# Window attention and a factored convolution, two layers in one kernel: a second layout for the value table, and the statistics rows loaded one unit later

## The chip, the cores and the metric

The kernel runs on one core of one Trainium2 chip. The metric is the device time of one execution in microseconds (us). Three executions of the kernel before gave 2969.43, 2971.66 and 2973.84 us; their median, 2971.66 us, is the time before.

## The reference, cut to what matters

The input x has 2 images of 128 channels and 256 x 256 pixels, float32. Two layers follow each other, each with a group norm in front and a residual around it:

```
x = x + attention(gn(x))          # layer 0
x = x + convolutions(gn(x))       # layer 1
```

`gn` takes mean and variance over 4 channels and the whole image, so an image's statistics must be complete before its first row can be normalised. The attention cuts the image into windows of 8 x 8 pixels (the queries) and reads keys and values from the 12 x 12 pixels around each (the 8 x 8 and a border of 2), with 4 heads of 32 channels, a relative position term, and a mask:

```
qkv  = W_qkv @ gn(x)
q    = 8x8 windows of q;  k, v = 12x12 windows of k, v (stride 8)
attn = softmax(q k^T * scale + rel_pos(q) + mask)     # mask: -inf unless row and column offset are both odd
out  = W_out @ (attn v)
```

The mask lets a query see only those keys whose row and column differ from its own by odd numbers. The kernel uses that: it splits rows and columns by parity and computes only what the mask leaves. Layer 1 (a 5 x 1 convolution, a 3 x 1 channelwise one, a product with a 1 x 3 dilated one) is not touched by the change.

## The kernel before, in words

An image is cut into 32 strips of 8 rows. A strip is worked on in two *units*, one for each row parity r; unit u belongs to strip k = u // 2 and parity r = u % 2. Two images give 64 strips and 128 units. A strip's 256 columns are 32 windows, taken as 16 pairs (`NPAIR = 16`); the column parity is called c. Below, an *even unit* has r = 0, an *odd unit* r = 1, and the two units of one strip are a *pair of units*.

Layer 0 (`attention_fast`) emits its instructions under a manual schedule: for each of the five engines (TensorE, VectorE, ScalarE, GpSimd, SyncE) the order in which the code emits is the order in which the engine runs. Only semaphores, set by the framework from what each instruction reads and writes, hold an instruction back. The loop over u emits in this order:

- even unit: `load_rows(k + 2)` (L316, the rows of a later strip, 10 rows = 1280 KB); odd unit: `normalise(k + 2)` (L356 on VectorE);
- in the first image, at the even units 2, 4, ... 58: `input_stats(u)` (L128 `bn_stats` on VectorE over 8 or 10 rows of the second image, tile `f_sx`) and right after it `load_next()` (L305, the next 8 or 10 rows of the second image into the same single buffer `f_sx`). The second image's group norm is thereby prepared during the first;
- `biases(u)` (L562) and `scores(u)` (L579) on TensorE, the exponentials on ScalarE (L589);
- `keys(u + 1)` (L382, `f_pk`), `coefficients` (L473, L482, L486);
- `attend(u)`: for each of 16 window pairs and 4 heads one matmul (L605, `f_o`), whose moving operand is a slice of the value table `f_vt`: 128 keys, 2 column parities, 33 values (32 channels and a 1 that gives the softmax's denominator);
- in an odd unit: `bring(1, ...)`; `turn(u)`;
- in an even unit: `values(k + 1)` (L495, `f_pv`, 4 groups of 4 matmuls into the row buffer `f_vn`, copied at L500) and `bring(0, ...)`; in an odd unit: the queries of the next two units (L445, L447, `f_pq`);
- `project(u)` (L382, `f_py`; L639 adds the residual; L643 stores the result of the unit, 512 KB, to DRAM).

All of layer 0's loads and stores are issued by SyncE (SPq in the profile), in the order emitted. Its completion counters are eight, used in rotation: in the compiled order each transfer waits for the one issued eight places before it, besides what its buffers ask for.

The value table. `f_vn` holds a strip's value rows, one partition for each of 128 pixel positions (32 for each of r and c), all 16 window pairs behind each other in the free dimension: 16 x 4 heads x 33 floats = 8,448 bytes. `f_vt[r]` holds, for one row parity, the keys of a window: partitions 0 to 63 for column parity 0, 64 to 127 for column parity 1, and the other column parity's places stay zero, so that one matmul gives both column parities side by side. `bring(r, pieces)` moves a strip's rows from `f_vn` to `f_vt[r]` with DMAs from SBUF to SBUF: for each c and piece, the rows themselves (L525), and the two border columns, taken from the neighbouring pair (L529, L532). A window's 6 key rows of one parity lie in a ring, so a strip's 4 rows are one piece (4 rows) in two strips out of three and two pieces (2 and 2) in the third. `bring` thus issues 6 DMAs in two strips out of three and 12 in the third; I call the pairs of units *light* and *heavy* for it. `bring_top` (L542, L546, L549) does the same for the two rows above an image's first strip.

TensorE's program is fully unrolled; matmuls in float32 appear in the profile as two weight loads (PEld) and two matmuls (PE) each. `PIECES` and `pieces(u)` cut some matmuls into parts and are the same in both kernels.

The shape of the table and the order of its dimensions are one line (L221), the place of the load another (L685):

```
vt = [cst.tile([P, NPAIR, 2, HEADS, 33], F32, ...) for r in range(2)]
...
if u == 0 or u in stats_at:
    load_next()
```

Of the kernel before, what the change touches and what calls it, by code (L numbers as in the profile page):

```python
# [10 lines left out]
F32 = mybir.dt.float32  # L11
# [9 lines left out]
P = 128  # L21
W = 256
HEADS = 4
# [4 lines left out]
NPAIR = 16  # L28
# [159 lines left out]
def attention_fast(tc, io, x1_d, norm, st_x, st_y, tags, ends, weights, both, layer1):  # L188

    nc = tc.nc  # L190
# [4 lines left out]
    with ExitStack() as l0:  # L195
        cst = l0.enter_context(tc.tile_pool(name="f_cst", bufs=1))
# [21 lines left out]
        xo = [t[:, 2048:2560].rearrange("p (n r c j) -> p n r c j", n=NPAIR, r=2, c=2) for t in xt]  # L218
        tops = {}
        kt = [cst.tile([P, 2, NPAIR * NKEY + 4], F32, tag=f"f_kt{r}", name=f"f_kt{r}") for r in range(2)]  # L220
        vt = [cst.tile([P, NPAIR, 2, HEADS, 33], F32, tag=f"f_vt{r}", name=f"f_vt{r}") for r in range(2)]  # L221
        vn = both.sb.tile([P, NPAIR, HEADS, 33], F32, tag="vn", name="f_vn")

        sc = [
# [6 lines left out]
        for r in range(2):  # L231
            nc.gpsimd.memset(kt[r], 0.0)
            nc.gpsimd.memset(vt[r], 0.0)
            for c in range(2):
                nc.gpsimd.memset(vt[r][64 * c : 64 * c + 64, :, c, :, 32:33], 1.0)
        nc.gpsimd.memset(vn[..., 32:33], 1.0)
        nc.gpsimd.memset(wb, 0.0)

# [43 lines left out]
        stats_at, norm_at = {}, {}  # L282
        quarter_at = {}
        for b in range(NB - 1):
            row = 0
            for i in range(NS - 3):
                n = 10 if i < 12 else 8
# [23 lines left out]
        def load_rows(k):  # L311

            b, s = divmod(k, NS)
            t = rawp.tile([P, 10, W], F32, tag="raw", name=f"f_raw_{k}")
            n = min(10, H - 8 * s)
            nc.sync.dma_start(t[:, 0:n, :], x[b, :, 8 * s : 8 * s + n, :])  # L316
            raws[k] = t

        def slots_of(k):

            first = (4 * k + 2) % 6
            return [(0, 4, first)] if first < 4 else [(0, 2, 4), (2, 2, 0)]
# [195 lines left out]
        def bring(r, pieces):  # L518

            end = NPAIR - 1  # L520
            for c in range(2):
                at, to = 32 * (2 * r + c), 64 * c
                for i, m, slot in pieces:
                    lo = at + 8 * i
                    nc.sync.dma_start(  # L525
                        vt[r][to + 8 * slot : to + 8 * (slot + m), :, c], vn[lo : lo + 8 * m]
                    )
                    first = to + 48 + 2 * slot
                    nc.sync.dma_start(  # L529
                        vt[r][first : first + 2 * m - 1 : 2, 1:NPAIR, c], vn[lo + 7 : lo + 8 * m : 8, 0:end]  # L530
                    )
                    nc.sync.dma_start(  # L532
                        vt[r][first + 1 : first + 2 * m : 2, 0:end, c], vn[lo : lo + 8 * m - 7 : 8, 1:NPAIR]
                    )

        def bring_top(r, b):

            v, slot = tops[b][2], 4 * NS * b % 6
            for c in range(2):
                for odd in range(2):  # L540
                    lo, to = 64 * odd + 16 * (2 * r + c), 64 * c
                    nc.sync.dma_start(  # L542
                        vt[r][to + 8 * slot : to + 8 * slot + 16, odd:NPAIR:2, c], v[lo : lo + 16]
                    )
                    first = to + 48 + 2 * slot
                    nc.sync.dma_start(  # L546
                        vt[r][first : first + 3 : 2, odd + 1 : NPAIR : 2, c], v[lo + 7 : lo + 16 : 8, 0 : 8 - odd]
                    )
                    nc.sync.dma_start(  # L549
                        vt[r][first + 1 : first + 4 : 2, 1 - odd : NPAIR - 1 : 2, c],  # L550
                        v[lo : lo + 9 : 8, 1 - odd : 8],
                    )

# [40 lines left out]
        def attend(u):  # L594
            p = pts.pop(u)
            ons[0] = on = wk.tile([P, 2, NPAIR, 32], F32, tag="on", name=f"f_on_{u}", bufs=1)
            k, r = divmod(u, 2)
            if r == 0:
                rcs[0] = wk.tile([P, 2, NPAIR, 2, 1], F32, tag="rc", name=f"f_rc_{k}")
            for lo, hi in ((0, 6), (6, 11), (11, NPAIR)):  # L600
                bank = ps_pj.tile([P, 512], F32, tag="pj", name=f"f_o_{u}_{lo}")
                po = bank[:, 0 : 66 * (hi - lo)].rearrange("p (n c d) -> p n c d", c=2, d=33)
                for n in range(lo, hi):
                    for h in range(HEADS):
                        nc.tensor.matmul(  # L605
                            po[32 * h : 32 * h + 32, n - lo], p[:, h // 2, n, h % 2],
                            vt[r][:, n, :, h], start=True, stop=True,
                        )

                rc = rcs[0][:, r, lo:hi]  # L610
                nc.vector.reciprocal(rc, po[:, :, :, 32:33])
                nc.vector.tensor_tensor(
                    on[:, :, lo:hi].rearrange("p c n d -> p n c d"), po[:, :, :, 0:32],
                    rc.to_broadcast([P, hi - lo, 2, 32]), ALU.mult,
                )
# [35 lines left out]
        def emit(parts):  # L651
            for f in parts:
                f()
# [4 lines left out]
        with tc.manual_schedule(engines=ORDERED):  # L658
            normalise(0)
            emit(keys(0, ONE, ONE))  # L660
            top_values(0)
            bring_top(0, 0)
            values(0, range(4))
            for r in range(2):
                bring(r, slots_of(0))
            bring_top(1, 0)
            by_place(0, (0, 4))
            coefficients(0, 0)
            coefficients(0, 1)
            normalise(1)  # L670
            by_place(1, (0, 2))
            for u in range(2):
                emit(queries(u, ONE, ONE))
            for u in range(NU):
                k, r = divmod(u, 2)
                b, s = divmod(k, NS)
                later, more = u + 1 < NU, k + 1 < NB * NS
                if r == 0:
                    if k + 2 < NB * NS:
                        load_rows(k + 2)  # L680
                elif k + 2 < NB * NS:
                    normalise(k + 2)
                if u in stats_at:
                    input_stats(u)
                if u == 0 or u in stats_at:  # L685
                    load_next()
                step = lambda: None
                if u in norm_at:
                    st, i, name = norm_at[u]
                    steps = norm.steps(st[i], ps_pj, name, last=False)  # L690
                    step = lambda: next(steps)
                if u == 8:
                    weights.sums()
                if u in (NU - 4, NU - 2, NU - 1):
                    next(layer1)
                biases(u)
                scores(u, pieces(u)[3])
                step()
                step()
                at_top = more and (k + 1) % NS == 0  # L700
                cuts = pieces(u)[0]
                if later:
                    emit(keys(u + 1, cuts, cuts))
                step()
                step()
                if more:
                    coefficients(k + 1, r)
                elif later:
                    next(layer1)
                step()  # L710
                attend(u)
                if more and r == 1:
                    bring(1, slots_of(k + 1))
                    if at_top:
                        bring_top(1, b + 1)
                if not later:
                    next(layer1)
                turn(u)
                step()
                if r == 0 and more:  # L720
                    if at_top:
                        top_values(b + 1)
                        bring_top(0, b + 1)
                    values(k + 1, range(4))
                    bring(0, slots_of(k + 1))
                elif later and more:
                    cuts = pieces(u)[1]
                    emit(queries(u + 1, cuts, cuts) + queries(u + 2, cuts, cuts))
                if more and r == 0:
                    by_place(k + 1, (2, 4))  # L730
                elif k + 2 < NB * NS:
                    by_place(k + 2, (0, 2))
                if u > 0:
                    result_stats(u - 1)
                project(u)
                if u in quarter_at:
                    st, i, name, part = quarter_at[u]
                    norm.quarter(st[i], name, part)
                del qs[u]
            result_stats(NU - 1)  # L740
# [966 lines left out]
```

## Time and profile before

| What | Value |
|---|---|
| median of 3 executions | 2971.66 us |
| profiled execution, its own time | 2972.91 us |
| span in that profile (first to last instruction) | 2971.0 us |
| granted TensorE clock | 0.994 |
| PE busy | 2785.4 us (94%) |
| DVE busy | 2136.9 us (72%) |
| ACT busy | 1509.7 us (51%) |
| POOL busy | 640.7 us (22%) |
| layer 0's first `f_o` matmul / last | 119.5 us / 1973.5 us |

The profile is of one execution, 1.9 us longer than its span and 1.25 us over the median. Up to about 91 us the statistics of the first image are loaded; the units of the first image run from about 112 to 1069 us, those of the second to 1976 us, layer 1 from there on. A line of the view of waits reads: engine, what it was about to do, what ended the wait, then total us, number of times and the longest. "issue" stands for idle time for which the profile shows no wait on anything. A line of the timeline reads: start, duration, engine, line of code, operation, tiles, number of instructions merged, and in brackets the idle time before it.

### The profile page before, as it was taken

The page shows a single profiled execution, that of the slowest core. Times are in us where ns is not written, and L with a number is a line of the kernel's source. Part 1 is how long each engine was busy: PE and PEld are TensorE (multiplying, and loading weights), DVE is VectorE, ACT ScalarE, POOL GpSimd, SP SyncE. Part 2 cuts the span into 40 slices and gives each one's busy share as a digit, 9 for nine tenths or more (in the row PEclk, how much of TensorE's full clock was granted, in tenths as well). Part 3 has the DMA queues.
Part 4 walks back from the last instruction along what each step waited for, and adds up shares of the span by engine and source line. Part 5 has one row for each costly group of instructions (what it writes and reads, how often), then busy time and mean ns, then how long its engine had stood idle before and what let it go on. Part 6 is the DMA issues. An engine that isn't in the chain of part 4 may idle for free.

```text
span 2971.0 us, 117385 instructions
## 1 busy us (share of the span) xinstructions
PE 2785.4 (94%) x51762; PEld 2109.1 (71%) x51762; DVE 2136.9 (72%) x3601; ACT 1509.7 (51%) x2379; POOL 640.7 (22%) x2049
## 2 busy tenths in 40 slices
PE   0699999999999999999999999999999999999998
PEld 0588888888888888989888899864444444444443
DVE  8566666666666655655556565569999999999997
ACT  0345454445444545445454554546666666666654
POOL 1233322233332332332333323300000000000000
PEclk9999999999999999999999999999999999999999
DMA  9666655566555455455454555448888878888885
GB/s 394 197 185 176 173 163 170 161 174 175 157 169 158 134 127 135 123 136 126 134 146 120 137 128 138 123 123 216 217 221 216 213 212 215 220 217 216 218 217 148
DMA packets 309396, 521.83 MB, mean 176 GB/s; under 512 B 20784, under 2 KB 259856, under 8 KB 276752
## 3 DMA queue, kind: packets, MB, share of 16 engines
q1 hardware_dynamic: 299808, 448.17, 51.0%
q0 software_dynamic: 9072, 66.06, 11.9%
q8 instruction: 412, 6.75, 0.9%
q14 instruction: 104, 0.85, 0.1%
HBM read 284.78 MB, written 134.22 MB: 141 GB/s over the span
## 4 chain that ended last, share of the span: by engine, by line
PE 76%; issue 19%; SPq 1%; POOL 1%; DMA 1%; DVE 1%; ACT 1%; POOLq 0%; DVEq 0%; ACTq 0%
PE f_s L579 9%; PE f_o L605 9%; PE f_pk L382 8%; PE f_pv L495 8%; PE f_py L382 8%; PE a_o L887 6%; PE a_e L887 6%; PE f_pq L447 6%; PE f_pa L473 4%; PE f_s L562 4%; PE f_pq L445 2%; PE a_d L938 2%; PE a_c L887 1%; PE b L980 1%; PE g L867 1%
## 5 line engine op out<-in xcount | busy, mean ns | idle before, releaser
L486 DVE TENSOR_SCALAR f_cf<-f_pa,f_keep 128x512 f32<-128x512 f32 x128 | 103.7, 810 | 546.8 <-ACT f_cf L482 546.7
L589 ACT ACTIVATE f_p<-f_s 128x512 f32<-128x512 f32 x512 | 265.4, 602 | 442.7 <-PE f_s L579 442.0
L453 ACT ACTIVATE f_q<-f_pq,f_head 128x512 f32<-128x512 f32 x512 | 303.1, 702 | 153.8 <-PE f_pq L447 153.8
L396 POOL COPY f_kt<-f_kt 128x60 f32<-128x60 f32 (+1 forms) x348 | 105.8, 340 | 1262.4 <-ACT f_kt L410 1238.6
L373 POOL COPY f_xq<-f_xn 128x96 f32<-128x96 f32 x1024 | 333.2, 356 | 12.3 <-DVE f_xn L356 12.3
L962 ACT ACTIVATE t<-t,w 128x1024 f32<-128x1024 f32 x127 | 145.9, 1149 | 368.2 <-DVE t L955 363.0
L969 DVE SCALAR_TENSOR_TENSOR t<-t,w,t 128x1024 f32<-128x1024 f32 x254 | 325.9, 1283 | 7.3 <-ACT t L962 1.3
L605 PE MATMUL f_o<-f_vt,f_p 128*32 128x66 f32 x16384 | 280.1, 222 | 34.2 <-issue 33.9
L579 PEld LDWEIGHTS f_s<-f_q,f_kt 64*64 64x64 f32 x17176 | 275.0, 133 | 52.0 <-issue 51.7
L579 PE MATMUL f_s<-f_q,f_kt 64*64 64x64 f32 (+1 forms) x17176 | 293.9, 221 | 1.5 <-issue 1.1
L605 PEld LDWEIGHTS f_o<-f_vt,f_p 128*32 128x32 f32 x16384 | 250.9, 109 | 50.8 <-issue 41.2
L495 PE MATMUL f_pv<-f_wqkvT,f_xn 128*128 128x128 f32 x2048 | 251.7, 280 | 24.0 <-issue 22.9
L495 PEld LDWEIGHTS f_pv<-f_wqkvT,f_xn 128*128 128x128 f32 x2048 | 236.2, 192 | 32.4 <-issue 25.9
L382 PE MATMUL f_pk<-f_xn,f_wqkvT 128*128 128x192 f32 (+3 forms) x1496 | 257.3, 321 | 0.7 <-ACT f_kt L410 0.7
L382 PE MATMUL f_py<-f_ot,f_woT 128*128 128x160 f32 (+1 forms) x1520 | 248.5, 313 | 7.0 <-issue 5.0
L998 POOL DMA_DIRECT2D y<-f_x x63 | 54.5, 866 | 919.1 <-DVE y L990 871.2
L887 PE MATMUL a_o<-xm,w1s 128*128 128x512 f32 x512 | 242.3, 594 | 4.5 <-ACT t L878 4.5
L887 PE MATMUL a_e<-xm,w1s 128*128 128x512 f32 x512 | 240.7, 591 | 0.0
L382 PEld LDWEIGHTS f_py<-f_ot,f_woT 128*128 128x128 f32 x1520 | 230.7, 192 | 11.6 <-issue 8.8
L382 PEld LDWEIGHTS f_pk<-f_xn,f_wqkvT 128*128 128x128 f32 x1496 | 221.3, 190 | 12.6 <-issue 1.7
L447 PE MATMUL f_pq<-f_xn,f_wq_s 128*128 128x192 f32 (+1 forms) x1008 | 210.2, 331 | 0.0
L500 ACT COPY f_vn<-f_pv 128x512 f32<-128x512 f32 x128 | 75.0, 586 | 263.2 <-PE f_pv L495 245.0
(149 smaller groups left out, 4782.8 us busy)
## 6 DMA issues: line engine op xcount, KB each, us to landing
f_raw<-in_x SPq DMA_DIRECT2D x62, 1280.0 KB
f_x<-f_x SPq DMA_DIRECT2D x128, 512.0 KB
y<-f_x POOLq DMA_DIRECT2D x63, 1024.0 KB, 7.9
out<-y SPq DMA_DIRECT2D x63, 1024.0 KB
f_sx<-in_x SPq DMA_DIRECT2D x49, 1024.0 KB
f_vt<-f_vn SPq DMA_DIRECT2D x172, 264.0 KB
raw<-f_x SPq DMA_DIRECT2D x64, 640.0 KB
raw<-f_x SPq DMA_DIRECT2D x62, 384.0 KB
```

The source lines that it names most:

```text
L373: nc.gpsimd.tensor_copy(xq[:, half, t2, 1:4, :, c].rearrange("p t r n e -> p r t n e"), xn[k % 2][:, windows, :, c, 0:3, t2:8:4].rearrange ...
L382: nc.tensor.matmul(dst[:, 512 * lo // last : 512 * hi // last], w, moving[:, n * lo // last : n * hi // last], start=True, stop=True,)
L447: nc.tensor.matmul(by_pair[:, lo:hi, 8:32], wq_s, xn[k % 2][:, lo:hi, r, c, 0:3].rearrange("p n i j -> p n (i j)"), start=True, stop=True,)
L453: nc.scalar.activation(q[:, c, :, i].rearrange("p n (j t) -> p n j t", t=4), pq.rearrange("p (n t j) -> p n j t", n=NPAIR, t=4), AF.Copy, ...
L473: nc.tensor.matmul(pa[64 * half : 64 * half + 64, 64 * t : 64 * t + 64], wb[:, t2, t1].rearrange("p h x -> p (h x)"), xq[:, half, t2, t1]. ...
L495: nc.tensor.matmul(pv[:, P * n : P * n + P], xn[k % 2][:, 4 * g + n].rearrange("p r c i j -> p (r c i j)"), wvT, start=True, stop=True,)
L579: nc.tensor.matmul(sc[g][n // 8][64 * c : 64 * c + 64, n % 8, lo:hi].rearrange("p i x -> p (i x)"), kt[r][rows, c, NKEY * n : NKEY * n + 6 ...
L589: nc.scalar.activation(pts[u][:, g, 8 * half : 8 * half + 8].rearrange("p n i x -> p (n i x)"), sc[g][half].rearrange("p n i x -> p (n i x ...
L605: nc.tensor.matmul(po[32 * h : 32 * h + 32, n - lo], p[:, h // 2, n, h % 2], vt[r][:, n, :, h], start=True, stop=True,)
L887: nc.tensor.matmul(pa[:, : n * W], w, rows, start=i == 0, stop=i == len(terms) - 1)
L962: nc.scalar.activation(t3[:, j : j + 4], t1[:, j : j + 4, :], AF.Copy, scale=w3[:, 0:1])
L969: nc.vector.scalar_tensor_tensor(t3[:, j : j + 4], t1[:, j + tap : j + tap + 4, :], w3[:, tap : tap + 1], t3[:, j : j + 4], ALU.mult, ALU.add,
```

## The change

Two edits. First, the value table's dimensions "pair" and "column parity" change places: from `[P, NPAIR, 2, HEADS, 33]` to `[P, 2, NPAIR, HEADS, 33]`. In the old order the 16 pairs of one column parity lie 1,056 bytes apart in a partition, in runs of 528 bytes; in the new order they lie behind each other. The matmul's slice follows: its two column parities now lie 8,448 bytes apart and no longer 528. Second, `load_next()` is called in the unit after one with statistics (3, 5, ... 59; in the last there is nothing left to load) and no longer in the unit itself. Neither the order nor the number of compute instructions differs, and the DMAs are as many as before.

```diff
-        vt = [cst.tile([P, NPAIR, 2, HEADS, 33], F32, tag=f"f_vt{r}", name=f"f_vt{r}") for r in range(2)]
+        vt = [cst.tile([P, 2, NPAIR, HEADS, 33], F32, tag=f"f_vt{r}", name=f"f_vt{r}") for r in range(2)]
...
-                nc.gpsimd.memset(vt[r][64 * c : 64 * c + 64, :, c, :, 32:33], 1.0)
+                nc.gpsimd.memset(vt[r][64 * c : 64 * c + 64, c, :, :, 32:33], 1.0)
...
         def bring(r, pieces):
...
-                        vt[r][to + 8 * slot : to + 8 * (slot + m), :, c], vn[lo : lo + 8 * m]
+                        vt[r][to + 8 * slot : to + 8 * (slot + m), c], vn[lo : lo + 8 * m]
...
-                        vt[r][first : first + 2 * m - 1 : 2, 1:NPAIR, c], vn[lo + 7 : lo + 8 * m : 8, 0:end]
+                        vt[r][first : first + 2 * m - 1 : 2, c, 1:NPAIR], vn[lo + 7 : lo + 8 * m : 8, 0:end]
...
-                        vt[r][first + 1 : first + 2 * m : 2, 0:end, c], vn[lo : lo + 8 * m - 7 : 8, 1:NPAIR]
+                        vt[r][first + 1 : first + 2 * m : 2, c, 0:end], vn[lo : lo + 8 * m - 7 : 8, 1:NPAIR]
...
         def bring_top(r, b):
...
-                        vt[r][to + 8 * slot : to + 8 * slot + 16, odd:NPAIR:2, c], v[lo : lo + 16]
+                        vt[r][to + 8 * slot : to + 8 * slot + 16, c, odd:NPAIR:2], v[lo : lo + 16]
...
         def attend(u):
...
-                            vt[r][:, n, :, h], start=True, stop=True,
+                            vt[r][:, :, n, h], start=True, stop=True,
...
-                if u == 0 or u in stats_at:
+                if u == 0 or u - 1 in stats_at:
                     load_next()
```

More of the change, by code (lines that the diff above doesn't have):

```diff
@@ L546, in bring_top @@
                     nc.sync.dma_start(
-                        vt[r][first : first + 3 : 2, odd + 1 : NPAIR : 2, c], v[lo + 7 : lo + 16 : 8, 0 : 8 - odd]
+                        vt[r][first : first + 3 : 2, c, odd + 1 : NPAIR : 2], v[lo + 7 : lo + 16 : 8, 0 : 8 - odd]
                     )
                     nc.sync.dma_start(
-                        vt[r][first + 1 : first + 4 : 2, 1 - odd : NPAIR - 1 : 2, c],
+                        vt[r][first + 1 : first + 4 : 2, c, 1 - odd : NPAIR - 1 : 2],
                         v[lo : lo + 9 : 8, 1 - odd : 8],
```

## The prediction, made before the changed kernel ran

> **What bounds the kernel now.** I read the page first: TensorE (PE) is the bound, and from the third of 40 slices on it is nearly full. What can be gained in layer 0 lies in PE's idle time after 130 us; the 91 us of loading ahead of it are not touched.
>
> ```profile
> PE 2785.4 (94%) x51762; PEld 2109.1 (71%) x51762; DVE 2136.9 (72%) x3601; ACT 1509.7 (51%) x2379; POOL 640.7 (22%) x2049
> PE   0699999999999999999999999999999999999998
> q1 hardware_dynamic: 299808, 448.17, 51.0%
> q8 instruction: 412, 6.75, 0.9%
> ```
>
> The view of waits for PE says what this idle time is. Over the whole run:
>
> ```profile
> PE f_o L605 <- issue: 33.9, 41, 2.3
> PE f_pv L495 <- issue: 22.9, 19, 2.2
> PE f_pq L445 <- DVE f_cf L486: 7.9, 2, 5.5
> PE f_py L382 <- issue: 5.0, 8, 1.3
> ```
>
> The reader is to see that these are some 60 us with no semaphore to blame. Split into stretches, the first image (115 to 590 and 590 to 1070 us) and then the second (1070 to 1550 and 1550 to 1990) differ in one thing. The first pair of lines below is 115:590, the second 590:1070:
>
> ```profile
> PE f_pv L495 <- issue: 15.8, 12, 2.2
> PE f_o L605 <- issue: 6.4, 9, 2.2
> ...
> PE f_o L605 <- issue: 7.1, 9, 2.0
> PE f_pv L495 <- issue: 5.9, 6, 1.7
> ```
>
> and the second image, 1070:1550 and 1550:1990:
>
> ```profile
> PE f_o L605 <- issue: 10.9, 11, 2.3
> PE f_pv L495 <- issue: 1.1, 1, 1.1
> ...
> PE f_o L605 <- issue: 9.5, 12, 2.0
> PE f_py L382 <- issue: 3.3, 5, 1.3
> ```
>
> The f_o stalls are in both images (13.5 us, then 20.4), the f_pv stalls only in the first: 21.7 us against 1.1, or 6.1 with f_py (1.7 in 1070:1550 and the 3.3 shown), where the same block of instructions ends in the second image. The first image alone has statistics loads. The timeline shows such a stall in the middle of a run of like matmuls, where no semaphore stands:
>
> ```profile
> 416.75 1.69 PE L605 MATMUL f_o<-f_vt,f_p 128*32 128x66 f32 x100 [0.30 <-issue]
> 418.37 3.17 PE L495 MATMUL f_pv<-f_wqkvT,f_xn 128*128 128x128 f32 x26
> 422.93 0.83 PE L495 MATMUL f_pv<-f_wqkvT,f_xn 128*128 128x128 f32 x6 [1.39 <-issue]
> ```
>
> From one stall to the next are 100 + 26 matmuls and as many weight loads, 252 instructions. And in nearly every pair of units the stalls sit in the even unit, in which SyncE has just issued two loads, the strip rows and the statistics rows:
>
> ```profile
> 410.99 0.63 SPq L316 DMA_DIRECT2D f_raw<-in_x  x1
> 413.32 0.33 SPq L305 DMA_DIRECT2D f_sx<-in_x  x1
> ```
>
> So I read the stall as PE waiting for its next 256 instructions. The trace's DMA packet records bear this out. Queue q8 carried 412 packets of 16 KB; PE's 103,524 matmuls and weight loads and 1,572 semaphore instructions are 410.5 times 256. The packets of these two loads ran from 413.3 to 421.3 us; instruction packets ran at 414.53 to 415.50 and 420.51 to 421.51, and PE went on at 416.75 and 422.93, 1.25 and 1.42 us after their ends. After the block boundary at 416.75 the fetch began 3.8 us later. In odd units, with no load in flight, it begins 0.8 to 2 us after the boundary and PE does not stop.
>
> **What the Trainium skill says.** "Runtime: NRT & Kernel Launch", section Instruction fetch mechanics: instructions are streamed in blocks of 16 KiB, 256 instructions, and the cost of a boundary is "mostly hidden". The block size agrees (412 packets); hidden it is not here, at up to 2.3 us a time. "DMA: Bandwidth & Descriptors", section Queues, rings and completion order: each DMA engine goes round robin between the rings it has work for, a packet at a time. The trace agrees in part: the fetch gets in before a burst is over, but late. The same page, Why small descriptors are slow, says that transfers within SBUF don't suffer from small descriptors. The trace disagrees: the 528-byte packets, all but a few from f_vn to f_vt, take 46.8 ns on average, 11 bytes/ns, and 8,192-byte ones on the same queue 368 ns, 22 bytes/ns.
>
> **The change part by part.**
>
> *Value table.* The run of 16 pairs becomes one run of 8,448 bytes (7,920 for the border columns). The trace has 164,320 packets of 528 bytes; 2,528 belong to bring_top, whose source skips every other pair, and stay. The other 161,792 (7,574 us of engine time at 46.8 ns) become 10,240 long ones. At the 368 ns of an 8,192-byte packet, scaled with size, that is about 3,840 us. So q1's share falls by 3,730/(16 x 2971) = 8 points, to about 43%. What is it worth to PE? The bring bursts (425.9 to 434.4 us, 435.6 to 444.0) lie mostly in odd units and between them, where PE has no stall, so I take 0. The work that hides it is two units' time, some 29 us, between a bring and the attend that reads it; without that cover a bring's 4 to 8 us would show. Bounds: the freed engines could shorten f_o stalls (at best half of 33.9, 17 us), or longer packets could delay fetches in odd units, as in the third rival. SyncE's issue time is 0.62 us a DMA whatever its shape and stays; the L532 issues, median 872 ns, may come down to the 621 of L525, off the path.
>
> *The matmul's slice* has 66 columns in two runs before and after. Nothing in the trace has another stride on this operand, so its cost is bounded by 0 on both sides unless the runs' distance counts; I take 0 and look at the 219 ns of L605. The four memsets of ones (0.21 us each) are at the start under the loading.
>
> *Statistics load leaves even units.* The DMAs queued behind it on SyncE, bring(0) and the store, move up by one issue, 0.33 us, and lose SyncE's waits for bn_stats (24.4 us in all, covered: bring(0) waits for f_vn ten us later anyway). On PE the f_pv stalls fall to what the second image has: 21.7 - 6.1 = 15.6 us gained. One piece of evidence from the first image itself: the last load is issued at 941.0 us; the next heavy pair has no such load and stalls 0.24 us at 978.87, where earlier heavy ones lost 1.0 to 2.2. f_o stalls stay: the strip rows are issued first, and these stalls are as long without a statistics load.
>
> *It comes into odd units*, 29 loads less the first, between the even unit's store (L643) and bring(1). In a light pair (store issued at 458.85) it would be issued near 459.5, with packets from 461.8 (2.3 us from issue to packet, as at 410.99) to about 466 (4 us for 8 rows). PE's boundaries are near 462.1 (a fifth into f_o) and 467.1 (the end of f_pq). A fetch must have begun by about 464.8 (1 us for the packet and 1.35 to PE's restart), 2.7 us after the boundary; in even units f_o to f_pv leaves 2.3. Under strip rows alone, the even unit's fetch is late by 1 us (stalls of 0.3) or, in a quarter of the cases, by 3 (stalls of 2). With the larger margin the first is free and the second costs about 1 us: 0.25 us a load. In a heavy pair the load would go out near 433.5, its packets from 436 to 440; the fetch at 439.13 is then up to 1 us late with about 0.3 to spare. I take 0.25 us again: 28 x 0.25 = 7 us lost. Bounds: 0, and 28 x 1.2 = 34 us if each stalls as an f_pv did (21.7/18).
>
> *The wait that it adds.* By the rotation of eight counters, the eighth DMA of a heavy bring(1) waits for the statistics load to land (near 441 us, its turn at 439); behind it on SyncE are four more brings, the store and the next strip load, about 2 us late. The store's buffer is wanted at the next L639, the brings by the next L500 copy, both over 3 us later: 0. VectorE wants the rows at 439.95: up to 1.5 us late, and VectorE idles 3.46 us before the f_cf that PE needs: 0; in light pairs they land some 3 us early.
>
> *Sum:* -15.6 + 7 = -8.6 us. The profiled execution's 2972.91 us becomes 2964.3; on the median, 1.25 lower, 2963.
>
> **Rivals.** *The stall only moves*: odd units lose what even ones gain, 0.55 us a load: 2971. For: the margin is only 0.4 us larger. Against: a single burst there, two now.
>
> *The compact table helps PE as well*: strip rows no longer share engines with late bring packets, f_o stalls halve: -8.6 - 17 = -25.6, 2946. For: f_o holds most of the stalls. Against: in light pairs the bring burst ends at 410.4, before the strip rows' first packet at 413.3.
>
> *Slower*: long packets in odd units. Statistics rows and 8,448-byte table rows meet in the same rings just after f_o's boundary, and each load stalls PE 1.2 us there: 34 - 15.6 = +18, 2990. It decides from 0.55 us a load, and is measurable from (15.6 + 6)/28 = 0.77. For: fetches were late only beside 8 and 10 KB packets, never beside 528-byte ones. Against: bring(1) issues one row per engine each 0.65 us or so, which leaves gaps.
>
> **How the numbers follow.** 0.2%, 6 us, is about what a measurement of this kernel can tell from no change. Forecast 0.47 (0.42 faster, 0.05 within), moved 0.24 (0.20 within, 0.04 slower), table helps too 0.12 (faster), slower 0.17. So faster 0.54, same 0.25, slower 0.21. The range runs from 2950 (all 21.7 us gone, nothing lost) to 2982 (0.9 us lost a load: 26 - 15.6 = +10); most of the slower case and half of the table's lie outside, under 0.2. The forecast's own range is 2956 to 2968.
>
> **What would show it.** Right: waits of PE in 115:1070 with f_pv under 8 us, f_o near 13.5, new stalls in odd units (f_pq, f_py, or f_s after them) under 10; second image unchanged within 5 us; q1 near 43%; L605 at 219 ns. Wrong: new odd-unit stalls over 15 us; f_o stalls that shrink in the second image, where only the table changed; a longer L605.

## The result and the profile after

The changed kernel takes 2961.39 us (median of 20 executions), the kernel before in the same sessions 2971.51 us. The ratio is 0.9967, with a 95% interval of 0.9955 to 0.9978: about 10 us faster, where 8.6 had been forecast. The profiled execution has a span of 2960.0 us, against 2971.0.

The total came out near the forecast. Its two parts did not. The view of waits for PE in the first image (115 to 1070 us) of the changed kernel:

```profile
PE f_s L579 <- issue: 19.3, 10, 4.0
PE f_pq L445 <- issue: 14.6, 8, 3.2
PE f_o L605 <- issue: 11.1, 15, 1.6
PE f_pv L495 <- issue: 4.9, 4, 2.2
PE f_pq L447 <- issue: 3.0, 5, 0.9
```

The f_pv stalls have gone as forecast, from 21.7 us to 4.9. But where 7 us were to come back through the loads in odd units, f_s and f_pq have 36.9; 3.2 of these are one stall in unit 1, ahead of the first moved load, and 33.7 are left for the loads. In the second image (1070 to 1990), where only the table changed and nothing was to happen:

```profile
PE f_o L605 <- issue: 14.5, 19, 4.1
```

The f_o stalls fell from 20.4 us, and the f_py ones, 5.0 before, are gone. Of the 14.5 us, 4.1 are one stall at the change of images, where the kernel before waited 5.5 us for VectorE; without it 10.4 are left, half of what there was.

Waits do not hold everything. The clock records show TensorE's granted clock at half, mostly for 3.41 us at a time, which costs 1.7 us each. In layer 0 of the kernel before and the changed one 12 of the 14 such stretches begin within 1.5 us of the end of a stall of 1.7 us or more; that the stall brings them on is my reading, not shown by a run of its own.

So I count in units. From the instruction records I take the first bias matmul (L562) of each unit; from one to the next a unit that never stalls takes 13.70 us in every kernel of the table below. The time over that, summed, is a kernel's loss in layer 0. I leave out the first two units, the change of images (61 to 65) and the last four. "After a heavy bring(1)" are the even units that follow an odd one with 12 brings.

| us over 13.70 a unit | 1st image: even, other | even, after a heavy bring(1) | odd | 2nd image: even | odd |
|---|---|---|---|---|---|
| before | 35.5 | 18.6 | 1.3 | 36.7 | 2.5 |
| changed | 12.8 | 36.3 | 20.8 | 15.0 | 0.4 |
| table_only | 25.3 | 11.0 | 0.4 | 16.0 | 0.5 |
| load_only | 18.5 | 46.9 | 50.4 | 46.3 | 2.6 |
| table_padded | 33.0 | 18.5 | 1.3 | 48.4 | 2.0 |
| table_no_rows | 3.8 | 1.4 | 0.5 | 16.6 | 0.8 |
| table_slow | 19.2 | 9.5 | 0.3 | 20.5 | 3.2 |
| small_rows | 36.5 | 13.8 | 0.4 | 24.6 | 0.6 |
| odd_pool | 10.0 | 0.8 | 40.7 | 15.7 | 0.4 |
| odd_light | 22.6 | 0.4 | 24.7 | 17.2 | 0.5 |
| heavy_pool | 16.9 | 27.6 | 20.5 | 17.4 | 0.5 |
| table_split | 7.5 | 18.3 | 3.5 | 20.3 | 0.5 |
| table_split_light | 20.3 | 9.9 | 4.1 | 18.4 | 0.5 |

(The experiments are told below.) From before to changed the first image lost 14.5 us and the second won 23.8. With 2 us won at the change of images and 0.7 lost at the start (the first two units lose 3.7, the last ones win as much), layer 0 ends 10.7 us earlier by the same records (last unit begins at 1956.0 and not at 1966.7).

Half-clock time is part of these losses: of the first image's, 5.1 us before, 11.9 changed, 25.6 in load_only and none in table_only. Each line is one profile, and kernels whose second image is the same code scatter: its two columns sum to 39 to 50 us with short rows (before, load_only, table_padded) and to 15 to 21 with long ones, table_slow and small_rows apart. The gap between the two groups is clear, a few us within one are not.

The page's DMA lines after the change:

```profile
DMA packets 157844, 521.83 MB, mean 176 GB/s; under 512 B 20784, under 2 KB 98064, under 8 KB 117008
q1 hardware_dynamic: 148256, 448.17, 51.3%
```

Half of the packets are gone, and the queue's share of the engines' time is where it was, 51.0% before. The issues, min/median/max in ns, in the tile view of f_vt:

```profile
L525 SPq DMA_DIRECT2D f_vt<-f_vn x340: 535/536/1223, 113.0 to 1940.3; - x170
L529 SPq DMA_DIRECT2D f_vt<-f_vn x340: 577/592/847, 113.6 to 1940.9; - x170
L532 SPq DMA_DIRECT2D f_vt<-f_vn x340: 562/585/1110, 114.3 to 1941.5; - x170
L605 PE MATMUL f_o<-f_vt,f_p x16384: 217/219/319, 120.2 to 1962.8; 128*32 128x66 f32 x200
```

The matmul has its 219 ns as before. SyncE issues faster: medians 536, 592 and 585 ns for 621, 647 and 872.

### The profile page after: what moved, and what is told of

Read it like the earlier page. It is cut to its first block, busy times and chain, and to the rows that moved or that the text cites. A ratio compares the mean times of both kernels' runs of the same rounds, so it can differ in the third digit from the quotient of the medians.

```text
span 2960.0 us, 117321 instructions
## 1 busy us (share of the span) xinstructions
PE 2780.9 (94%) x51762; PEld 2106.9 (71%) x51762; DVE 2136.9 (72%) x3601; ACT 1511.8 (51%) x2379; POOL 641.1 (22%) x2049
## 3 DMA queue, kind: packets, MB, share of 16 engines
q1 hardware_dynamic: 148256, 448.17, 51.3%
q0 software_dynamic: 9072, 66.06, 11.9%
## 4 chain that ended last, share of the span: by engine, by line
PE 92%; issue 5%; DVE 1%; ACT 1%; POOL 1%; DMA 1%; SPq 0%; DVEq 0%; ACTq 0%; POOLq 0%
PE a_o L887 11%; PE a_e L887 11%; PE f_s L579 9%; PE f_o L605 8%; PE f_pk L382 8%; PE f_pv L495 8%; PE f_py L382 8%; PE f_pq L447 6%; PE f_pa L473 5%; PE f_s L562 5%; PE a_d L938 4%; PE f_pq L445 2%; PE b L980 2%; PE a_c L887 2%; PE g L867 2%
## 5 line engine op out<-in xcount | busy, mean ns | idle before, releaser
L579 PE MATMUL f_s<-f_q,f_kt 64*64 64x64 f32 (+1 forms) x17176 | 293.8, 222 | 19.3 <-issue 19.3
L605 PE MATMUL f_o<-f_vt,f_p 128*32 128x66 f32 x16384 | 273.0, 220 | 25.7 <-issue 25.6
L382 PEld LDWEIGHTS f_pk<-f_xn,f_wqkvT 128*128 128x128 f32 x1496 | 224.7, 192 | 12.9 <-issue 1.7
L612 DVE TENSOR_TENSOR f_on<-f_o,f_rc 128x320 f32<-128x320 f32 (+1 forms) x384 | 197.1, 513 | 13.3
```

The lines of the kernel that those rows point to most:

```text
L382: nc.tensor.matmul(dst[:, 512 * lo // last : 512 * hi // last], w, moving[:, n * lo // last : n * hi // last], start=True, stop=True,)
L579: nc.tensor.matmul(sc[g][n // 8][64 * c : 64 * c + 64, n % 8, lo:hi].rearrange("p i x -> p (i x)"), kt[r][rows, c, NKEY * n : NKEY * n + 6 ...
L605: nc.tensor.matmul(po[32 * h : 32 * h + 32, n - lo], p[:, h // 2, n, h % 2], vt[r][:, :, n, h], start=True, stop=True,)
L612: nc.vector.tensor_tensor(on[:, :, lo:hi].rearrange("p c n d -> p n c d"), po[:, :, :, 0:32], rc.to_broadcast([P, hi - lo, 2, 32]), ALU.mult,)
```

## The experiments

Theory A, formed from these two traces: the long rows gave the whole gain, and the load's move took part of it back. Theory B is the prediction: the table is worth nothing, the move gave the gain. Ratios are to the kernel before in the same session; its median was between 2971.5 and 2975.6 us, so a few us between runs of two sessions tell nothing.

**table_only** is the changed kernel with the load where it was.

```diff
-                if u == 0 or u - 1 in stats_at:
+                if u == 0 or u in stats_at:
```

> Only the value table has the new order; the statistics rows are loaded in even units as before. Theory A (the long rows gave the whole gain, the moved load cost about 14 us in the first image, as the two traces read): the second image keeps its 25 us, the first gains too, 2930 to 2945 us. Theory B (as predicted: the table is worth nothing, the load's move gave the gain): 2971 us.

Measured: 2932.24 us, ratio 0.9855 (0.9833 to 0.9876). A. The view of waits from 115 to 1070 us, its first image and, from 1037 us, the start of the second:

```profile
PE f_pv L495 <- issue: 27.8, 27, 1.7
PE f_o L605 <- issue: 7.4, 6, 4.4
```

The f_pv stalls stay, as the load in even units should have it, but the rest has shrunk: 4.4 of the 7.4 us of f_o are one stall in the second image, at its unit 65, so the first image has 3.0 where the kernel before had 13.5.

**load_only** is the kernel before with the load moved.

```diff
-                if u == 0 or u in stats_at:
+                if u == 0 or u - 1 in stats_at:
```

> Only the statistics load moves to odd units; the table is as before. Theory A: slower than before by 10 to 20 us, 2981 to 2991 us, with stalls of f_s and f_pq in odd units. Theory B: 2963 us.

Measured: 3035.92 us, ratio 1.0204 (1.0181 to 1.0226): A's direction, at three to six times its size. The move costs 63 us with the old table and 29 us with the new one (2961.39 less 2932.24; two sessions, whose kernels before lay 1.4 us apart). The edits are not additive; with the long rows the move does half the damage. A third of the first image's extra loss in load_only (60 us by the table) is half-clock time, 25.6 us against 5.1 before. Its waits:

```profile
PE f_pq L445 <- issue: 26.1, 10, 6.0
PE f_s L579 <- issue: 25.3, 15, 4.0
PE f_pq L447 <- issue: 15.3, 9, 2.5
```

**table_padded** asks what of the table does it.

```diff
-        vt = [cst.tile([P, 2, NPAIR, HEADS, 33], F32, ...) for r in range(2)]
+        vw = [cst.tile([P, 2, NPAIR, HEADS * 33 + 1], F32, ...) for r in range(2)]
+        vt = [t[..., 0 : HEADS * 33].rearrange("p c n (h d) -> p c n h d", d=33) for t in vw]
```

> The table in the new order, but one float of padding after each pair's 132, so that every transfer is again 16 runs of 528 bytes; load as before. If the long runs (fewer packets, shorter issues) give the gain: as before, 2971 us within 6. If the order of the dimensions itself does it, through the matmul's operand: as table_only.

Measured: 2979.07 us, 1.0021 (1.0009 to 1.0032), 299,808 packets on q1 again: some 6 us slower than before. With the new order but short runs nothing is gained; the long runs do it.

**table_slow**: long runs also shorten SyncE's issues. This gives that time back.

```diff
+            for _ in range(2):
+                nc.sync.dma_start(idle[turns[0] % 4][0:1], io["c_keep"][0:1])
+                turns[0] += 1
```

> table_only, with two 16-byte DMAs of a constant into unused tiles after each bring, so that SyncE spends about 1 us more on each bring, as it did with the short runs (raw rows of heavy pairs issued near 4.6 us into the unit again and not at 2.7). If the issue time is what the long runs saved: back to 2960 to 2975 us. If it is the packets themselves: 2932 to 2940 us.

Measured: 2936.89 us, 0.9868 (0.9840 to 0.9895). In the second image the strip rows after a heavy bring(1) were issued 4.0 us into the unit (median; before 4.6, table_only 2.7), so most of the delay was restored, and 2 to 5 us of the 40 came back, within the two intervals. By the table this hides 7 us lost in the second image (of the 23 that table_only had won there) and 8 won in the first. The issue time is thus a small part of the total, and perhaps a third of the second image's gain. Where no heavy bring(1) goes ahead, the strip rows are issued 1.6 us into the unit in all three kernels, and in those even units the second image still loses 25.7 us before and 13.2 in table_only. By elimination the larger part is what the short packets do in the DMA engines.

**table_no_rows** prices the statistics loads.

```diff
-                if u == 0 or u in stats_at:
+                if u == 0:
...
-            norm.chunk(st_x[b], row // 2, sxs.pop(u))
+            norm.chunk(st_x[b], row // 2, sxs[2][:, 0:n])
```

> The new table, and of the 29 loads of statistics rows only the first; all 29 statistics read those rows, so 28 loads of about 1 MB are left out and the second image's statistics are of the wrong rows. It prices the loads wherever they stand. Theory A: the first image stalls as little as the second does in the changed kernel, some 0.5 us a pair of units, 2905 to 2920 us. Theory B (loads in odd units nearly free): not over 8 us under the changed kernel once the table is worth nothing, about 2955 us.

Measured: 2898.82 us, 0.9747 (0.9729 to 0.9766), 6 us under A's range. With the new table the 28 loads cost 33 us in even units and 63 us in odd ones (the latter from two sessions).

**small_rows** asks how a load holds a fetch up.

```diff
-            t = rawp.tile([P, 10, W], F32, tag="raw", ...)
+            t = rawp.tile([P, 2570], F32, tag="raw", ...)
+            t = t.rearrange("p (a w) -> p a w", w=W + 1)[:, :, 0:W]
```

(and likewise the statistics rows, 512 floats and one of padding)

> table_only, with one float of padding after every 256 floats of a strip row and after every 512 of a statistics row, so that these loads go in packets of 1 KB and 2 KB and no longer 10 and 8 KB. If an instruction fetch waits for a number of packets, and long ones hold it up: the stalls of f_o and f_pv shrink to under 15 us, 2895 to 2910 us. If it waits for bytes or for the backlog as a whole: 2930 to 2940 us.

Measured: 2955.95 us, 0.9931 (0.9905 to 0.9956). Both were wrong: short packets made it 21 to 24 us slower than table_only. In the first image's even units 30 to 54 the load burst ends at 12.3 us into the unit and not at 11.4 (medians), and the fetch that follows f_o's block begins at 10.55 and not at 10.04. Here a fetch does not slip in between short packets: in both kernels it begins only 1.3 to 1.7 us before the burst ends. Part of the longer burst is the packets' own rate: 20.0 bytes/ns for those of 1,024 bytes, 23.5 for those of 10,240 in table_only (means).

**table_shift** tests that these stalls are instruction fetches at all.

```diff
+                if u == 2:
+                    spare = ps_pj.tile([P, 512], F32, tag="pj", name="f_spare")
+                    for i in range(16):
+                        nc.tensor.matmul(spare[:, 4 * i : 4 * i + 4], wq_s, wvT[:, 0:4], start=True, stop=True)
```

> table_only, with 16 matmuls of 4 columns into an unread tile put once ahead of unit 2: 64 more instructions for TensorE, 2 to 3 us of its time, and everything after stands 64 instructions later in its blocks of 256. If the unexplained stalls are waits for the next block, each moves 32 matmuls forward in the program: from f_o with about 100 of 128 left to f_pa near its end, from f_pv with about 6 of 32 left to f_o with about 6 left. If they come from the matmuls themselves or their data: they stay at f_o x100 and f_pv x6. Time: 2925 to 2950 us either way.

Measured: 3283.59 us, 1.1055 (1.1027 to 1.1083). The places moved as the fetch theory said: in the first image's even units the stalls now stand at f_pa with 1 to 4 matmuls left (15 times) and at f_o with 1 to 7 left (31 times). The time I had not foreseen. Its waits and its timeline:

```profile
PE f_o L605 <- issue: 230.5, 121, 4.3
PE f_pv L495 <- issue: 38.1, 24, 3.5
PE f_pa L473 <- issue: 7.0, 18, 1.2
```

```profile
521.25 2.04 PE L605 MATMUL f_o<-f_vt,f_p 128*32 128x66 f32 x124 [0.17 <-PE f_pa L473]
527.50 0.31 PE L605 MATMUL f_o<-f_vt,f_p 128*32 128x66 f32 x4 [4.21 <-issue]
```

In 95 of the 121 stalls 1 to 13 of f_o's 128 matmuls are left, in odd units too. The reader is to see what the block boundary's place is worth. In the other kernels it falls a fifth into f_o, so that f_o's 256 instructions, issued in 2 us, are spread over two blocks of some 4.7 us each. Here one block is nearly all f_o and lasts about 2.3 us, less than a fetch takes with no load in flight, and PE stops 121 times in 128 units. 64 instructions out of 105,000 cost 351 us against table_only; 82 of them are half-clock time (95 us in this profile, 12 in table_only's).

**odd_pool** and **odd_light** ask why even units after a heavy bring(1) lose 36 us in the changed kernel. SyncE's view of waits there has a line that the kernel before does not have:

```profile
SPq L529 <- DMA f_sx<-in_x: 44.9, 10, 7.2
```

That is the wait of the eighth bring for the statistics load.

```diff
-                nc.sync.dma_start(sxs[u], x[b, :, row : row + n, :])
+                nc.gpsimd.dma_start(sxs[u], x[b, :, row : row + n, :])
```

> The changed kernel, with the statistics load issued by GpSimd at the same place and no longer by SyncE. On SyncE nothing then waits for it to land by the rotation of eight counters. If that wait (and the late strip load behind it) makes the 36 us of stalls in even units of heavy pairs: those fall under 12 us, 2932 to 2942 us. If the load's own burst makes them: 2958 to 2965 us, as the changed kernel.

```diff
-                if u == 0 or u - 1 in stats_at:
+                if u == 0 or (u in stats_at and u % 6 == 2) or (u - 1 in stats_at and u % 6 != 3):
```

> The changed kernel, except that in heavy pairs the statistics load stays in the even unit. If the wait of the eighth bring for that load is what costs in heavy pairs: stalls in heavy pairs of the first image fall from 43 us to about 11 (as in table_only), 2930 to 2936 us. If the load would cost the same there anyhow: 2955 to 2962 us.

Measured: odd_pool 2947.13 us, 0.9900 (0.9872 to 0.9928); odd_light 2936.88 us, 0.9883 (0.9862 to 0.9904). In both the 36 us fell to under 1 us, but in both the load's packets have also left that place: GpSimd reaches it 10.4 us into the even unit, 3.3 us before the odd one begins (odd units then lose 40.7 us), and odd_light issues it in the even unit before. They do not tell the wait from the burst.

**heavy_pool** was to do so: the load stays near its time, but off SyncE.

```diff
-                if u == 0 or u - 1 in stats_at:
+                if u == 0 or (u - 1 in stats_at and u % 6 != 3):
                     load_next()
...
                     emit(keys(u + 1, cuts, cuts))
+                if u - 1 in stats_at and u % 6 == 3:
+                    load_next(nc.gpsimd)
```

> The changed kernel, except that in the odd units with 12 brings GpSimd issues the statistics load, after the key copies, near the 7 us at which SyncE issued it: the burst stays about where it was, but no bring, store or strip load on SyncE waits for it to land. If that wait makes the 36 us of stalls in the even units that follow: they fall under 15 us, 2936 to 2945 us. If the burst does, by lying over an instruction fetch: they stay at 25 us or more, 2952 to 2962 us.

Measured: 2959.50 us, 0.9946 (0.9931 to 0.9961). 27.6 of the 36.3 us stay, as the burst would have it. But the run is not as clean as I took it to be. The wait for f_sx at L529 is gone, and another stands in its place: the transfer eight places before that bring is now the store, which lands late beside the same burst.

```profile
SPq L529 <- DMA f_x<-f_x: 21.4, 9, 5.3
```

The strip rows after a heavy bring(1) go out at 5.3 us into the unit, against 7.3 in the changed kernel and 2.7 in table_only (medians), so about half of the delay is still there, and the run alone doesn't bound what the wait costs. The DMA packet records say more. In heavy pairs the third fetch of the odd unit begins at 12.8 us in table_only and at 14.8 in the changed kernel (medians, first image). In the changed kernel's units 33 and 34 the load's packets run from 9.4 us into the odd unit to 14.8, the bring rows held up behind them to 15.9, and the fetch from 15.2 to 16.7. PE wants it 2.5 us into the even unit, which is 16.3 us on the same count, and f_s stops for 1.78 us. SyncE's turn at the waiting L529 comes only at 12.8, when table_only's fetch has already begun, and a wait that keeps transfers back puts nothing ahead of the fetch. By this reading the f_s stalls, 19.3 of the 24.2 us that PE stands idle in these even units, are the burst's, and another 8.5 us of the 36.3 are half-clock time. The f_pv stalls, the other 4.9 us, may come from the late strip rows; no run here tells. The timeline shows another such stop of f_s, at unit 28:

```profile
550.01 1.49 PE L579 MATMUL f_s<-f_q,f_kt 64*64 64x32 f32 x78
553.28 1.03 PE L579 MATMUL f_s<-f_q,f_kt 64*64 64x64 f32 x52 [1.77 <-issue]
```

**table_split** and **table_split_light** try shorter bursts.

```diff
-                nc.sync.dma_start(sxs[u], x[b, :, row : row + n, :])
+                nc.sync.dma_start(t[:, 0:4], x[b, :, row : row + 4, :])
+                rest.append((t[:, 4:n], x[b, :, row + 4 : row + n, :]))
...
+                if rest and r == 1:
+                    nc.sync.dma_start(*rest.pop())
```

> table_only, with the statistics load in two: 4 rows in the even unit, the rest in the odd one. If a fetch is late by as much of a burst as is still ahead of it, two halves cost less than one: 2910 to 2925 us. If every load in an odd unit costs as in the changed kernel (about 2 us a pair): 2950 to 2962 us.

> table_split, except that in heavy pairs the whole statistics load stays in the even unit. From the parts measured so far: light pairs 9 us of stalls as in table_split (table_only 25.6), heavy pairs 11 as in table_only (table_split 20): 2914 to 2920 us, the fastest that computes the reference. If the half loads' gain was chance: 2925 to 2932 us.

(its edit: `cut = n if u // 2 % 3 == 2 else 4` in place of the 4.)

Measured: 2924.78 us, 0.9826 (0.9800 to 0.9851), and 2921.72 us, 0.9836 (0.9818 to 0.9855). Both beat both kernels; neither is apart from table_only, whose interval overlaps theirs, nor from the other. In table_split_light the loss in other even units was 20.3 us where I had counted on 7.5, so what the halves gain is not settled.

## Why the prediction was right in its total and wrong in its terms

- *The bound, and what the stall is*: right. PE waits for its next block of 256 instructions; table_shift moved the stalls by 64 instructions and found them where they had to be.
- *"so I take 0"* for the table: wrong; this is the step that failed. It is worth 24 us in the second image and 40 us in the whole kernel. The reason I gave, "PE has no stall" where the bring bursts lie, looked for stalls at the burst and not at what the burst does to the fetches around it; and fetches are late beside 528-byte packets too, which a line of the third rival denies. In the second image's odd units the third fetch begins 13.7 us into the unit before and 12.9 after (medians), so the next block begins with less in hand before; and the strip rows after a heavy bring(1) are issued at 4.6 and 2.7 us. The late start and the late issue were both in the trace before. The rival "the compact table helps PE as well" had this: the second image's f_o stalls did halve, and it was more than the 17 us that the rival gave it.
- *q1's share falls to 43%*: wrong, it stayed at 51.3%. A row of 8,448 bytes took 791 ns on average, twice the 380 that I scaled from loads of 8,192 bytes; the table's long rows took 7,333 us of engine time where the short ones had taken 7,574. With it falls "The trace disagrees" on small packets within SBUF: I had set 528-byte packets within SBUF against 8,192-byte ones from or to DRAM. Within SBUF the 528-byte packets have 11.3 bytes/ns and the 8,448-byte ones 10.7.
- *Issue time "stays"*: it fell by 55 to 287 ns a DMA (medians); by table_slow this is worth 2 to 5 us in all.
- *f_pv stalls fall by 15.6 us*: right; by 16.8 (21.7 to 4.9).
- *"0.25 us a load"* in odd units: mis-sized. f_s and f_pq stalls took 33.7 us for 28 loads, 1.2 us each, the upper bound that I had given to the rival "slower". In light pairs the forecast stall at the end of f_pq came as placed. In heavy pairs the burst came about where I had it (issued 7.1 us into the unit where I had 8.1, packets from 9.4 us where I had 10.6). What was wrong is the fetch beside it: I had it "up to 1 us late with about 0.3 to spare", and it began 2.0 us later than in table_only (medians), with bring rows held up in front of it that I had not counted, so f_s stopped.
- *The added wait costs 0*: not shown. It was 4.5 us on average where I had 2, and holds back the strip rows to about 7 us into the unit. By the packet records the f_s stalls are not its doing; 4.9 us of f_pv stalls may be.
- The half-clock time after stalls is a term that the sum did not have: in the first image it rose from 5.1 to 11.9 us.
- The measured total is thus the sum of two errors of opposite sign, and near the forecast by luck: the load's move, forecast at -8.6, cost 29 us; the table, forecast at 0, gave 40. Two of the signs that I had named for being wrong both came: new odd-unit stalls over 15 us, and f_o stalls that shrank in the second image.

What stays open: why short packets delay fetches beyond the bursts' own time, and why in table_no_rows, where neither image has statistics loads in its units, the even units of the second image still lose 16.6 us and those of the first 5.2. One difference is on record: the block boundary in f_o's even units has 97 to 103 matmuls left in the first image of the kernel before and 91 to 97 in the second. Whether that makes it, no run here tells.

## What to carry to other kernels

When a fully unrolled program streams its instructions through the same DMA engines as its data, count instructions between stalls: if it is the block size, price every transfer by the fetch it lies over, where in the program the boundary falls, and how dense the block behind it is. Do not cost a rearranged transfer at nothing because no stall stands beside it; compare the start of the fetches that follow it. And when two edits come together, run each alone: here the two together were 10 us faster, alone 40 faster and 63 slower.

## What the runs showed of the hardware that I had not expected

- From SBUF to SBUF neither length nor place alone sets a packet's rate. In the changed kernel packets of 8,448 bytes took 791 ns (10.7 bytes/ns), the rate of the 528-byte ones before (46.8 ns, 11.3), but the border rows of 7,920 bytes, within SBUF too, took 416 ns (19.0), and packets of 8,192 bytes from or to DRAM on the same queue 379 ns (21.6). The 8,448-byte packets with at most four of the table's long rows in flight (117 of 8,192) took 432 ns, those with 13 or more 800.
- 64 more instructions for TensorE, at the wrong place, cost 351 us, and the mean granted clock fell from 0.996 to 0.971.
- A stall of TensorE may cost more than its idle time: in layer 0 of the kernel before and the changed one, 12 of 14 stretches at half the clock begin within 1.5 us of the end of a stall of 1.7 us or more.
- Shorter packets did not make a load less harmful: 1 and 2 KB packets in place of 10 and 8 KB let the burst end 0.9 us later and made the kernel 21 to 24 us slower.
